# A graph layer on one core: whether nodes lie in a chunk's reach is told from each chunk's first and last edge, in the prologue, and no longer from all edges in the first passes

## The chip, the core and the metric

The program runs on one core of one Trainium2 chip. TensorE (PE; its weight loads are shown apart as PEld), VectorE (DVE), ScalarE (ACT) and GpSimd (POOL) compute; SyncE (SP) issues most of the plain DMAs, and POOL issues the indirect ones, which gather rows by an index in SBUF. The metric is the time of one execution on the device in microseconds, and of several executions the median. The profile is of one execution of its own.

## What is computed

One layer of a graph network on 12500 nodes of 128 features, with 200000 edges sorted by their target node `dst`. For each edge a score is taken between the target's query and the source's key and damped by `exp(-edge_weight)`; each node keeps its 16 best edges, makes a softmax of them, and adds up the messages of their sources.

```python
h = jnp.maximum(_layernorm(x, axis=-1), 0.0)
Qv = h @ W_Q.T
Ku = h @ W_K.T
score = jnp.einsum('md,md->m', Qv[dst], Ku[src]) * (1.0 / np.sqrt(d))
score = score * jnp.exp(-DECAY_LAMBDA * edge_dt)
order = jnp.lexsort((-score, dst))
...
keep = rank < TOPK
...
alpha = w / jnp.where(denom[dst_s] > 0, denom[dst_s], 1.0)
msgs = h[src_s] @ W_msg.T
agg = jax.ops.segment_sum(alpha[:, None] * msgs, dst_s, num_segments=n, indices_are_sorted=True)
return x + jax.nn.relu(h @ W_self.T + agg)
```

## The kernel before

**Groups and chunks.** The 200000 edges are cut into 1563 chunks of 128 edges, and 14 chunks (`GC`) are a group; there are 112 groups (`G`). A group answers for the nodes whose last edge lies in its 14 chunks, at most 128 nodes that follow one another. As the edges of its last node may run on, it also looks at the first chunk of the next group, so that it works on 15 chunks (`NJ`). A group's edges lie 128 to a chunk, one edge on each partition.

**The reach of a chunk.** Within its group, chunk j is taken to hold edges of the 40 nodes (`WN`) from place 8 j - 16 on, and no others. This is true of ordinary inputs but not of all, and so it is tested: places are told in `rel`, a tile with one group on each partition and, for each of its edges, the place of the edge's node among the group's nodes (112 x 1920, bf16). `w0` holds 8 j - 16 for each chunk. `dlw` is a view of `pd`, which has the same turned, with an edge on each partition: the place less the chunk's start, for 112 groups x 15 chunks, which makes 1680 elements on each of 128 partitions.

**What the tests lead to.** Tests write counts into the columns of `bad` (prologue) and of its copy `badc`: a node with 40 edges or more (column 0), `dst` not sorted (1), a node out of its chunk's reach (2), a group with too many nodes (3). `all_checked` adds them over the partitions with a small product on PE and writes `any_i`. At the end of the program (L904) all engines read `any_i`: if it is not 0, a general and much slower loop does the whole layer again.

**Prologue.** It loads the edges and `x`, writes `h` row by row into `h_tab` in DRAM, turns the indices of the sources into `idx_all`, builds `rel`, `pd` and the counts (L390 to L450). Tiles that only the prologue needs are in the pool `ep`, which ends with it; the pool `win` of the passes then lies in its place, so the first instruction that writes there waits for the last one that used `ep` (on ACT this is L539). POOL starts to gather rows here: for the first four groups (`RAW`) from `x`, to be normalised later, and for the others from `h_tab`.

**Gathers.** `let_go(g, k)` releases the gathers of two chunks: DVE copies two columns of indices into a small tile `ix` (L191), and POOL issues one indirect DMA for each chunk, 128 rows of 512 bytes into the tile `hs` of the group (L176). There are 8 buffers for `hs`, so a group's first gather also waits until PE has added up the group eight before it (L696), the last to read that buffer.

**Passes.** A loop over i from -3 to 110 does the work in an order written out by hand, and the engines run it as it stands, each its own instructions in that order. In pass i the stages of different groups stand side by side: nodes loaded for group i + 3, edges spread and places made for i + 1 (`far_of` L558, `away` L581, `places` L585), scores of i (L605) and their spread over slots (`scores_in_slots`, L613), slots of i - 1 gathered by node on PE (L621), best 16 of i - 2 (`best`, L635 on; `on_edges`, L670 to L677), weights and sums of i - 3 (L685, L686, L696), output of i - 5 (L716). `let_go` calls lie between them (`more`), mostly for groups i + 4 and i + 5. In passes 0 to 2 rows of groups 2 and 3 are normalised besides (L200, L221, L241).

**Work put off.** `later` is a list of small pieces of work. At the end of each pass with i > 0 one is taken from it:

```python
            if i > 0 and later:
                later.pop(0)()
```

Before the change there are nine, for passes 1 to 9. The first six tell whether nodes lie out of reach (L459, L471 to L475), all on DVE and all over the 1680 elements; the seventh and eighth are the count of edges per node (L477, L478), the ninth is `all_checked` (L463 to L467). The first six need two tiles of their own in `win`, `own_n` and `dl_n`.

Of the kernel before, what the change touches and what calls it, by code (L numbers as in the profile page):

```python
# [10 lines left out]
F32 = mybir.dt.float32  # L11
# [4 lines left out]
OP = mybir.AluOpType  # L16
# [4 lines left out]
P = 128  # L21
# [10 lines left out]
NJ = GC + 1  # L32
# [3 lines left out]
WN = 40  # L36
HALO = 64
# [23 lines left out]
def bc(ap, n):  # L61

    return ap.unsqueeze(2).to_broadcast([ap.shape[0], ap.shape[1], n])
# [7 lines left out]
def bm(ap, n):  # L71

    return ap.unsqueeze(1).to_broadcast([ap.shape[0], n, ap.shape[1]])
# [3 lines left out]
def gnn_layer(  # L77
# [27 lines left out]
    nc = tc.nc  # L105
    N, D = x.shape
# [5 lines left out]
    G = -(-CH // GC)  # L112
    assert G > TAIL + 2
    EG = GC * P
# [3 lines left out]
    RR = -(-CH // CPR)  # L118
# [28 lines left out]
    rel = const.tile([RR, RW + P], BF16, name="rel")  # L147
# [8 lines left out]
    dlw = pd[:, 16:16 + NJ, :].rearrange("e j g -> e g j")  # L156
# [88 lines left out]
    w0 = rows_pool.tile([P, NJ], F32, name="w0")  # L245
# [16 lines left out]
    with tc.tile_pool(name="edges", bufs=1) as ep, ExitStack() as stage:  # L262
# [8 lines left out]
        bad = ep.tile([P, 4], F32, name="bad")  # L271
# [29 lines left out]
        xs, t = [], 0  # L301
# [21 lines left out]
        k = RF if REM else RF - 1  # L323
# [21 lines left out]
        for w in range(2):  # L345
# [4 lines left out]
                                           op0=OP.mult, op1=OP.subtract)  # L350
# [27 lines left out]
        for g in range(2):  # L378
# [18 lines left out]
                                op0=OP.add, op1=OP.max)  # L397
# [7 lines left out]
        dst_f = dst_r.bitcast(F32)  # L405
# [11 lines left out]
        bb = rows_pool.tile([P, 2, G], F32, name="bb")  # L417
        nc.vector.tensor_copy(bb, pb[:, 0:2 * G].rearrange("p (a g) -> p a g", a=2))

        for j0 in range(0, NJ, 4):  # L420
            j1 = min(j0 + 4, NJ)
            pt = bank("q", 3)
            for j in range(j0, j1):
# [10 lines left out]
                                       op0=OP.add, op1=OP.is_gt, accum_out=bad[0:RR, 1:2])  # L434
# [4 lines left out]
        nc.vector.tensor_scalar(flags[:, 1:2], row[:, 0, G - TAIL:G - TAIL + 1], float(N - XT), None, op0=OP.is_lt)  # L439
        nc.vector.tensor_scalar(flags[:, 2:3], row[:, 0, G - TAIL - 1:G - TAIL], float(N - P), None, op0=OP.is_gt)  # L440
        nc.vector.tensor_reduce(bad[0:1, 3:4], flags[:, 0:3], axis=AX.X, op=OP.add)
        badc = rows_pool.tile([P, 4], F32, name="badc")
        nc.vector.tensor_copy(badc, bad)
        let_go(RAW, 6)
# [5 lines left out]
        nc.vector.tensor_copy(idxo, t1)  # L450


    mid = (WN - 1) / 2
    own_n, dl = [], []

    def far_from_start():
        for t in (own_n, dl):
            t.append(win.tile([P, G, NJ], F32, bufs=1, name="own_n" if t is own_n else "dl_n"))
        nc.vector.tensor_tensor(dl[0], dlw, bm(w0, G), op=OP.add)  # L459

    def all_checked():
        pb = bank("x", 1)
        nc.tensor.matmul(pb[0:1, 0:4], lhsT=ones, rhs=badc, start=True, stop=True)  # L463
        total = rows_pool.tile([1, 1], F32, name="total")
        nc.vector.tensor_reduce(total, pb[0:1, 0:4], axis=AX.X, op=OP.add)
        nc.vector.tensor_scalar(any_i, total, 1.0, None, op0=OP.min)
        nc.vector.tensor_scalar(uns, pb[0:1, 1:2], 1.0, None, op0=OP.min)  # L467

    later += [
        far_from_start,  # L470
        lambda: nc.vector.tensor_tensor(own_n[0], dl[0], bc(bb[:, 1, :], NJ), op=OP.is_lt),  # L471
        lambda: nc.vector.scalar_tensor_tensor(own_n[0], dl[0], 0.0, own_n[0], op0=OP.is_ge, op1=OP.mult),
        lambda: nc.vector.tensor_scalar(dl[0], dlw, -mid, None, op0=OP.add),
        lambda: nc.vector.tensor_tensor(dl[0], dl[0], dl[0], op=OP.mult),
        lambda: nc.vector.scalar_tensor_tensor(own_n[0], dl[0], (mid + 0.25) ** 2, own_n[0], op0=OP.is_gt,  # L475
                                               op1=OP.mult, accum_out=badc[:, 2:3]),
        lambda: nc.vector.tensor_reduce(badc[:, 0:1], pd[:, 0:NJ, :], axis=AX.XY, op=OP.max),  # L477
        lambda: nc.vector.tensor_scalar(badc[:, 0:1], badc[:, 0:1], float(KM), None, op0=OP.is_ge),  # L478
        all_checked,
# [424 lines left out]
    with tc.tile_pool(name="gen", bufs=1) as gen, tc.If(nc.values_load(  # L904
# [46 lines left out]
        lo, hi, clo, chi = row[:, 0, 0:NT], row[:, 0, 1:NB], row[:, 1, 0:NT], row[:, 2, 0:NT]  # L951
# [125 lines left out]
```

## Time and profile before

| | |
|---|---|
| median of 3 runs | 2030.86 us (2030.07 to 2034.2) |
| profiled execution | 2036.32 us, its span 2034.5 us |
| granted TensorE clock, mean | 0.915 |
| DVE busy | 1284.9 us, 63% |
| ACT busy | 1021.7 us, 50% |
| gathers (L176) from `h_tab` | 1507, first at 94.0 us, last at 1991.1 us |
| L459, one operation at 138.2 us | 3.23 us |
| L471, L472, L474, L475, one each from 156.2 to 212.4 us | 1.90 us each |
| L473, at 182.6 us | 1.71 us |
| L477, at 227.3 us | 1.90 us |

Times are microseconds from the span's start. In a list of groups, a line tells the program's line, the engine, the operation, the tile written and the tiles read, the shape, the count, then the busy time and the mean of one in ns, and the idle time of the engine just before these instructions with what ended most of it. "issue" as the cause means that the engine waited for nothing that the profile shows. In a timeline, a line has the start, the duration, engine, line, operation and tiles, and in brackets the idle time before it and what ended that.

### The profile page before, as it was taken

What the parts mean: (1) busy time and instruction counts of PE and PEld (TensorE: products, weight loads), DVE (VectorE), ACT (ScalarE), POOL (GpSimd) and SP (SyncE); (2) the same over time, 40 slices, a digit from 0 to 9 for tenths busy, and PEclk for the clock granted to TensorE, in tenths of its full rate; (3) what the DMA queues carried; (4) which work ended last, traced back from release to release, by engine and by line L of the source; (5) the groups of instructions that cost most, each with busy time, mean ns of one, the idle gap of its engine ahead of it and who ended that gap; (6) DMA issues with size and microseconds to landing.
All of it is one profiled execution on the core that took longest, in us unless ns stands there. A gap on an engine that the chain in (4) does not pass through costs nothing. (4 is left out here: it accounts for less than half of the span.)

```text
span 2034.5 us, 42215 instructions
## 1 busy us (share of the span) xinstructions
PE 1580.1 (78%) x13800; PEld 1303.9 (64%) x13801; DVE 1284.9 (63%) x7017; ACT 1021.7 (50%) x2190; POOL 1505.6 (74%) x1580
## 2 busy tenths in 40 slices
PE   0268899977878787888878787778878787878785
PEld 0147777766666666666666666666666666666664
DVE  7568877756656666666666566666666665666653
ACT  5765566544444454454444445444544444545440
POOL 6777777777777777777777777777777777777772
PEclk9979999998889899998888899898988888989987
DMA  9522222222222222222222222222222222222220
GB/s 220 179 59 56 76 69 69 66 64 66 65 65 66 65 64 63 66 65 65 66 65 66 66 65 64 64 64 65 66 66 65 65 66 66 66 64 64 64 58 19
DMA packets 101472, 143.46 MB, mean 71 GB/s; under 512 B 31063, under 2 KB 74327, under 8 KB 100480
## 3 DMA queue, kind: packets, MB, share of 16 engines
q0 software_dynamic: 50144, 102.74, 19.9%
q1 hardware_dynamic: 51102, 37.99, 6.8%
q8 instruction: 108, 1.77, 0.4%
q14 instruction: 118, 0.97, 0.2%
HBM read 126.79 MB, written 14.40 MB: 69 GB/s over the span
## 5 line engine op out<-in xcount | busy, mean ns | idle before, releaser
L176 POOL DMA_INDIRECT hs<-h_tab,ix x1507 | 1436.4, 953 | 461.9 <-issue 304.6
L605 DVE SCALAR_TENSOR_TENSOR prod<-hs,dec_all,q 128x128 f32<-128x128 f32 x1674 | 507.6, 344 | 296.2 <-DMA hs<-h_tab,ix 256.8
L558 ACT ACTIVATE far<-a,minus 128x512 bf16<-128x512 f32 (+1 forms) x447 | 294.3, 658 | 530.8 <-PE a L556 523.7
L596 PE MATMUL q<-q,to_e 128*128 128x128 f32 x3348 | 512.4, 301 | 0.0
L596 PEld LDWEIGHTS q<-q,to_e 128*128 128x128 f32 x3348 | 482.6, 213 | 33.5 <-DVE prod L605 13.7
L696 PE MATMUL e<-hs,alz 128*128 128x128 f32 x3240 | 419.1, 282 | 0.0
L696 PEld LDWEIGHTS e<-hs,alz 128*128 128x128 f32 x3240 | 377.9, 192 | 26.9 <-issue 19.2
L581 ACT ACTIVATE aw<-a 128x400 bf16<-128x400 f32 x336 | 169.1, 503 | 314.3 <-PE a L579 314.3
L635 DVE TENSOR_SCALAR ell<-slots,e 128x40 f32<-128x40 f32 x112 | 28.1, 251 | 357.1 <-PE e L621 304.6
L704 PE MATMUL s<-ident,agn 128*128 128x128 f32 x112 | 38.3, 342 | 262.8 <-DVE kept L685 260.8
L563 ACT ACTIVATE to_e<-far 128x1920 f32<-128x1920 bf16 x112 | 201.4, 1798 | 3.5
L556 PE MATMUL a<-rel,ident 112*128 112x512 bf16 (+1 forms) x447 | 195.0, 436 | 8.2 <-ACT far L558 8.1
L704 PEld LDWEIGHTS s<-ident,agn 128*128 128x128 f32 x112 | 17.0, 152 | 279.0 <-issue 274.7
L621 PE MATMUL e<-opo,sl 128*41 128x40 f32 x3348 | 194.0, 233 | 0.0
L621 PEld LDWEIGHTS e<-opo,sl 128*41 128x41 f32 x3348 | 180.1, 147 | 12.3
L605 DVE DVE_READ_ACCUMULATOR prod<-hs,dec_all,q 128x1 f32 x1674 | 138.4, 83 | 0.0
L585 ACT ACTIVATE opo<-aw 128x1200 f32<-128x1200 bf16 x112 | 134.2, 1198 | 0.1
L191 DVE COPY ix<-idx_all 128x2 int32<-128x2 int32 x754 | 133.2, 192 | 0.0
L579 PE MATMUL a<-minus_at,pdT 32*128 32x400 bf16 x336 | 115.4, 343 | 19.3 <-ACT pdT L572 9.6
L664 PE MATMUL x<-km,to_e 128*128 128x43 bf16 x1674 | 61.1, 183 | 66.7 <-DVE km L647 66.0
L664 PEld LDWEIGHTS <-to_e 128*128 128x128 bf16 x1674 | 49.7, 97 | 98.3 <-DVE km L647 96.7
L613 DVE TENSOR_TENSOR sl<-opo,s 128x600 f32<-128x600 f32 x112 | 87.6, 782 | 4.0
(179 smaller groups left out, 1678.0 us busy)
## 6 DMA issues: line engine op xcount, KB each, us to landing
hs<-h_tab,ix POOLq DMA_INDIRECT x1507
h_r<-h_tab SPq DMA_DIRECT2D x112, 64.0 KB
x_t<-in_x_dram SPq DMA_DIRECT2D x108, 64.0 KB
out_dram<-o SPq DMA_DIRECT2D x108, 64.0 KB
xg<-in_x_dram SPq DMA_DIRECT2D x2, 1400.0 KB
h_tab<-xg SPq DMA_DIRECT2D x2, 1400.0 KB
xg<-in_x_dram SPq DMA_DIRECT2D x1, 1120.0 KB
h_tab<-xg SPq DMA_DIRECT2D x1, 1120.0 KB
```

The lines of the kernel that those rows point to most:

```text
L176: nc.gpsimd.indirect_dma_start(out=T[g]["hs"][:, j, :], out_offset=None, in_=table[0:N, :], in_offset=bass.IndirectOffsetOnAxis(ap=index(j ...
L191: nc.vector.tensor_copy(ix[:, j0:j1], idx_all[:, GC * g + j0:GC * g + j1])
L556: nc.tensor.matmul(pr[:, 0:n1 - n0], lhsT=upper(ident[0:RR, g:g + 1]).to_broadcast([RR, P]), rhs=rel[:, n0:n1], start=True, stop=True)
L558: nc.scalar.activation(T[g]["far"][:, n0:n1], pr[:, 0:n1 - n0], AF.Square, bias=minus)
L563: nc.scalar.activation(T[g]["to_e"][:, 0:n], T[g]["far"][:, 0:n], AF.Relu, bias=1.0, scale=-1.0)
L579: nc.tensor.matmul(pr[:, 0:400], lhsT=T[g]["pdT"], rhs=minus_at.rearrange("k w j s -> k (w j s)")[:, n0:n1], start=True, stop=True)
L581: nc.scalar.activation(T[g]["aw"][:, n0:n1], pr[:, 0:400], AF.Square)
L585: nc.scalar.activation(T[g]["opo"].rearrange("e w j s -> e (w j s)"), T[g]["aw"], AF.Relu, bias=1.0, scale=-1.0)
L596: nc.tensor.matmul(pq[:, (j - j0) * P:(j - j0 + 1) * P], lhsT=T[g]["to_e"][:, j * P:(j + 1) * P], rhs=T[g]["q"], start=True, stop=True)
L605: nc.vector.scalar_tensor_tensor(prod, rows_of(g, j), dec_all[:, c:c + 1], T[g]["pq", b][:, (j % 4) * P:(j % 4 + 1) * P], op0=OP.mult, op1 ...
L621: nc.tensor.matmul(et[0:KM + 1, STEP * j:STEP * j + WN], lhsT=sl1[g % 2][:, j, :], rhs=T[g]["ow"][:, j, :], start=False, stop=(j == n - 1))
L696: nc.tensor.matmul(T[g]["pa"], lhsT=alz[g % 2][:, WW * j + PRE:WW * j + PRE + P], rhs=rows_of(g, j), start=(j == 0), stop=(j == n - 1))
```

## The change

The six operations on all edges go, and with them the tiles `own_n` and `dl_n`. In their place eleven small DVE operations stand in the prologue, between the other counts and the copy of `bad` to `badc`. As the edges are sorted, the places within a chunk never fall, so that the first and last edge of each chunk bound them. For each group (a partition) and chunk (15 elements) the new code takes the places of these two edges from `rel`, cuts them to the group's own nodes and the nodes that there are (`at_most`), and compares them with the chunk's start `w0` and with the start plus 40. Chunks that begin past the group's last node don't count. The number of chunks out of reach goes into column 2 of `bad`. The list `later` keeps three pieces, which are now due in passes 1, 2 and 3 and no longer in passes 7, 8 and 9.

```diff
         nc.vector.tensor_reduce(bad[0:1, 3:4], flags[:, 0:3], axis=AX.X, op=OP.add)
+        ends = rel.rearrange("g (j p) -> g j p", p=P)
+        lo, hi = ends[:, :, 0], ends[:, :, P - 1]
+        at_most = ep.tile([RR, 2], F32, name="at_most")
+        below, out_of = (ep.tile([RR, NJ], F32, name=f"out_of{k}") for k in range(2))
+        nc.vector.tensor_scalar(at_most[:, 0:1], dst_f[:, HALO - 1:HALO], -1.0, float(N - 2), op0=OP.mult, op1=OP.add)
+        nc.vector.tensor_copy(at_most[:, 1:2], rel[:, EG - 1:EG])
+        nc.vector.tensor_tensor(at_most[:, 0:1], at_most[:, 0:1], at_most[:, 1:2], op=OP.min)
+        nc.vector.tensor_scalar(out_of, hi, at_most[:, 0:1], None, op0=OP.min)
+        nc.vector.tensor_tensor(out_of, out_of, w0[0:RR, :], op=OP.subtract)
+        nc.vector.tensor_scalar(out_of, out_of, WN - 0.5, None, op0=OP.is_gt)
+        nc.vector.tensor_scalar(below, lo, 0.0, None, op0=OP.max)
+        nc.vector.tensor_tensor(below, below, w0[0:RR, :], op=OP.subtract)
+        nc.vector.scalar_tensor_tensor(out_of, below, 0.0, out_of, op0=OP.is_lt, op1=OP.max)
+        nc.vector.tensor_scalar(below, lo, at_most[:, 0:1], None, op0=OP.is_le)
+        nc.vector.scalar_tensor_tensor(out_of, out_of, 1.0, below, op0=OP.mult, op1=OP.mult,
+                                       accum_out=bad[0:RR, 2:3])
         badc = rows_pool.tile([P, 4], F32, name="badc")
         nc.vector.tensor_copy(badc, bad)
         let_go(RAW, 6)
...
-    mid = (WN - 1) / 2
-    own_n, dl = [], []
-
-    def far_from_start():
-        for t in (own_n, dl):
-            t.append(win.tile([P, G, NJ], F32, bufs=1, name="own_n" if t is own_n else "dl_n"))
-        nc.vector.tensor_tensor(dl[0], dlw, bm(w0, G), op=OP.add)
...
     later += [
-        far_from_start,
-        lambda: nc.vector.tensor_tensor(own_n[0], dl[0], bc(bb[:, 1, :], NJ), op=OP.is_lt),
-        lambda: nc.vector.scalar_tensor_tensor(own_n[0], dl[0], 0.0, own_n[0], op0=OP.is_ge, op1=OP.mult),
-        lambda: nc.vector.tensor_scalar(dl[0], dlw, -mid, None, op0=OP.add),
-        lambda: nc.vector.tensor_tensor(dl[0], dl[0], dl[0], op=OP.mult),
-        lambda: nc.vector.scalar_tensor_tensor(own_n[0], dl[0], (mid + 0.25) ** 2, own_n[0], op0=OP.is_gt,
-                                               op1=OP.mult, accum_out=badc[:, 2:3]),
         lambda: nc.vector.tensor_reduce(badc[:, 0:1], pd[:, 0:NJ, :], axis=AX.XY, op=OP.max),
         lambda: nc.vector.tensor_scalar(badc[:, 0:1], badc[:, 0:1], float(KM), None, op0=OP.is_ge),
         all_checked,
```

## The prediction

> **What bounds the kernel now.** I read the page's groups first, then the timeline of POOL, and only then the engines that feed it.
>
> ```profile
> PE 1580.1 (78%) x13800; PEld 1303.9 (64%) x13801; DVE 1284.9 (63%) x7017; ACT 1021.7 (50%) x2190; POOL 1505.6 (74%) x1580
> ...
> L176 POOL DMA_INDIRECT hs<-h_tab,ix x1507 | 1436.4, 953 | 461.9 <-issue 304.6
> ```
>
> PE is busier than POOL, but the busy share misleads. A gather (L176) takes 953 ns with 461.9 / 1507 = 0.31 us of idle before it that is put down to "issue", that is, to nothing but POOL itself. Together 1.25 us each. 1507 of them are 1898 us (1436.4 + 461.9), 93% of the span. The POOL timeline shows where this stream is not at that beat; the columns are start, duration, engine, line, operation, tiles and the idle time before it:
>
> ```profile
> 139.48 2.74 POOL L176 DMA_INDIRECT hs<-h_tab,ix  x1 [0.30 <-issue]
> ...
> 156.25 2.64 POOL L176 DMA_INDIRECT hs<-h_tab,ix  x1 [0.30 <-DVE hs L241]
> ...
> 166.71 0.94 POOL L176 DMA_INDIRECT hs<-h_tab,ix  x1 [0.30 <-issue]
> 168.91 1.19 POOL L176 DMA_INDIRECT hs<-h_tab,ix  x1 [1.25 <-PE a L579]
> 171.97 1.00 POOL L176 DMA_INDIRECT hs<-h_tab,ix  x1 [1.87 <-issue]
> ...
> 182.01 2.41 POOL L176 DMA_INDIRECT hs<-h_tab,ix  x1 [0.30 <-DVE prod L605]
> ...
> 197.75 2.42 POOL L176 DMA_INDIRECT hs<-h_tab,ix  x1 [0.30 <-DMA hs<-h_tab,ix]
> ...
> 213.51 1.58 POOL L176 DMA_INDIRECT hs<-h_tab,ix  x1 [0.30 <-issue]
> ```
>
> Two things are to be seen. Some gathers take 2.4 to 2.7 us and not 0.94. And after 171.97 no gather has more than 0.31 us of idle before it up to the last, at 1991.09: from there **POOL alone sets the time**. The stores at the end wait for DVE's work on the last gathered rows, a tail of 2034.5 - 1992.0 = 42.5 us that the change does not touch. So a microsecond taken from a gather after 169 us ends the program a microsecond earlier; one taken before 169 has to pass the wait of 1.25 us at 168.91. What stood beside the long gathers is in the timeline of DVE:
>
> ```profile
> 103.33 0.35 DVE L605 SCALAR_TENSOR_TENSOR prod<-hs,dec_all,q 128x128 f32<-128x128 f32 x1 [18.15 <-ACT opo L585]
> ...
> 138.22 3.23 DVE L459 TENSOR_TENSOR dl_n<-pd,w 128x1680 f32<-128x1680 bf16 x1
> ...
> 169.27 1.90 DVE L472 SCALAR_TENSOR_TENSOR own_n<-dl_n,own_n 128x1680 f32<-128x1680 f32 x1
> ```
>
> **What is removed.** Six operations on 1680 elements, one at the end of each of passes 1 to 6. Each with the gather beside it (start and duration from the two timelines), and what that gather lost against 0.94:
>
> - L459, 138.22, 3.23 us: gather 139.48 took 2.74, loss 1.80
> - L471, 156.18, 1.90: gather 156.25 took 2.64, loss 1.70
> - L472, 169.27, 1.90: the gather of 168.91 took 1.19 and the next began at 171.97; 171.97 - 168.91 - 1.25 = 1.81
> - L473, 182.59, 1.71: gather 182.01 took 2.41, loss 1.47
> - L474, 197.45, 1.90: gather 197.75 took 2.42, loss 1.48
> - L475, 212.38, 1.90: gather 213.51 took 1.58, loss 0.64
>
> The gathers end 0.8 us behind the end of the DVE operation (156.18 + 1.90 = 158.08 against 158.89; 199.35 against 200.17): they are held, not slowed. I take that as a shared path to SBUF.
>
> **The rule that speaks against it.** The Trainium skill, "SBUF — State Buffer", section "Who interferes with whom", says that a VectorE operation with two SBUF inputs contends with GpSimd's reads, but infers that it leaves descriptor generation alone, which needs the write side; its probe saw tensor_tensor stall no DMA. By that, five of the six (all with two inputs) cost POOL nothing, only L473 is left, and the sum is 1.47: 2029.4, no change. The rows say 2.64 and 2.42 beside just such operations, and 0.94 a few gathers on. I go by the rows. The same section says that a reduce never contends; I use that for L477 below, where the row is ambiguous.
>
> **What of it counts.** The first two losses, 3.50 us, lie before 168.91. That gather is the first of group 8 and takes group 0's buffer, so it must wait until PE has summed group 0:
>
> ```profile
> 166.31 2.05 PE L696 MATMUL e<-hs,alz 128*128 128x128 f32 x16
> 168.30 0.34 PE L579 MATMUL a<-minus_at,pdT 32*128 32x400 bf16 x1
> ```
>
> The sums end at 168.36 and the gather starts 0.55 later; POOL had been ready at 167.65 + 0.30 = 167.95. Are the sums earlier without L459 and L471? DVE was idle 0.94 us before 142.39 and 1.07 us before 160.05, waiting for PE (L621), just after these two operations; and the weights that the sums read were done at 158.98, 4.0 us before PE took them at 163.01. The chain runs through PE and ACT (ACT has one gap of 0.28 us from 141.11 to 149.97). So I count **nothing for L459 and L471**: the wait grows from 1.25 to 1.25 + 3.50 = about 4.8 us. The other four sum to 1.81 + 1.47 + 1.48 + 0.64 = **5.4 us**, all after the wait.
>
> Does POOL then run into the next wait? Group 9's first gather would come 14 x 1.25 = 17.5 after 168.91, at 186.4. Its index copy was done at 180.99, and PE's sums of group 1 before 181.76, when ACT had the product behind them: about 5 us of margin. The index copies of group 8's second and third pair were done at 169.36 and 172.29, and would be needed at 171.4 and 173.9. Passes 4 to 7 last 14.9 us with these operations and 13.3 without (start to start of L613), against 17.5 for POOL's 14 gathers, so the margin grows.
>
> Six shorter losses remain in the same stretch: 0.55, 0.57, 0.58, 0.48, 0.30 and 0.35 at 184.72, 211.70, 226.63, 229.71, 255.15 and 256.70, sum 2.83. The first four start within 0.2 us behind L613 or L686 (0.78 us, two inputs each), which stay, but at another time. In the ten passes from 257 to 390, at 13.3 us each, such losses sum to 0.36 + 0.18 + 0.45 + 0.44 = 1.43, or 0.14 a pass; six passes at that rate are 0.86 and the gain 2.0. At worst they fall as before, gain 0. I take the middle, 1.0.
>
> **What is added.** Eleven DVE operations on 1 or 15 elements a partition, before the copy to badc at 83.57. Rows near it: 0.17 for 14 elements (L219), 0.22 (L447), with 0.03 to 0.2 between dependent ones; so 0.14 to 0.24 each, about 2.2 us together (1.5 to 2.6). DVE then is idle for 18.15 us, so the cost is **zero**. Queued behind them: the index copy at 83.65, whose gather starts at 108.97; the other copies from 84.39, later still; and ACT's L539 at 89.75, the first to write where these tiles lay, which would have to wait for about 86.7. Without that idle time it would be 2.2 us. No DMA is added, and neither SP nor POOL is passed.
>
> **What is moved.** L477 (reduce, 1.90) goes from pass 7 to pass 1, in L459's place; there a loss of up to 1.8 on POOL would vanish in the wait. In pass 7 it stood beside a gather that lost 0.58, but L613 began 0.08 before that gather, as it did at 211.70 where L475 had not begun, so I have counted it with the short ones. L478 (0.15) goes to pass 2. The final sum, a small PE product and three DVE operations of 0.14 to 0.15, goes from pass 9 to pass 3: PE gets there at about 169.1, its bank having been read by 166.8, DVE is free at 169.3, so it waits for perhaps 0.1 and is done near 169.9, where L472 ended at 171.17. Zero.
>
> **Sum.** 5.4 + 1.0 = 6.4 us. The profiled execution took 2036.3 (span 2034.5), 5.5 above the median 2030.86; the terms are absolute and I take them off the median: **2024.5 us**. A difference of 0.2% (4.1 us) is about the least that can be told from none.
>
> **Rivals.**
>
> - *The early losses count too, 0.20.* If the sums of group 0 come earlier after all, up to 3.5 more, and with the short losses gone 5.4 + 2.8 + 3.5 = 11.7: 2019.2; its middle 2021.5. For it: the wait was only 0.96 too long. Against: DVE idles on PE just behind both operations.
> - *The loss comes back, 0.21.* The gathers lose their time in smaller pieces to L613, L675 and L686, which a compute loop of 13.3 us brings by more often, or the rule above holds: 0 to 4 gained, 2028.5. For it: short operations took 2.8 us in six passes. Against: only 1.4 in the next ten.
> - *A worse lock, 0.09, the slower side.* In the steady state a pass lasts as long as 14 gathers, 17.5 us, so L613 or L686 meets POOL at the same phase each time. Were that phase a bad one, each pass would lose 0.55. It eats the gain from 6.4 / 0.55 = 12 passes on, and is slower by 0.2% from 19; at 30 it is 2030.9 - 6.4 + 16.5 = 2041. Against: DVE's phase follows from the rows' landing, as before, where 1300 us cost POOL only 1.2.
> - *The new test flags the input* and the general path runs: below 0.01. For these inputs the farthest node lies 32 places past its chunk's start (limit 39) and the nearest 9 (limit 0), worked out from the reference's data.
>
> **Chances.** The forecast has 0.50, and of it 0.43 lie beyond 4.1 us. Faster: 0.43 + 0.20 = 0.63; same: 0.07 + 0.20 + 0.01 = 0.28; slower: 0.08 of the lock and 0.01 of the second rival, 0.09. The range from 2019.5 (nearly everything counts) to 2031 (nothing, with the spread of the shown runs, 2030.07 to 2034.2, in part) leaves out the lock and the last of the first rival.
>
> **What would show it.** Right: no gather over 1.6 us from 100 to 260 us; some 4.8 us of idle before the gather near 168.9, which starts where it did; the last gather at about 1991.1 - 6.4 = 1984.7, and an unchanged tail. Wrong: that gather starting well before 168; gathers of over 2 us beside other operations; many of 1.5 us after 400 us; a tail that is longer; ACT's L539 after 90 us.

## The result, and the profile after

| | before | after |
|---|---|---|
| median of 12 runs | 2031.65 us (2028.43 to 2035.7) | 2025.11 us (2021.62 to 2028.43) |
| ratio after / before, 95% interval | | 0.9964 (0.9956 to 0.9972) |
| profiled execution, its span | 2036.32, 2034.5 us | 2026.79, 2025.0 us |
| gathers, mean | 953 ns | 949 ns |

The change made the kernel 6.5 us faster by the medians; 2024.5 us had been forecast. The ratio is estimated from all executions and is not the quotient of the two medians: it makes 7.3 us, and its interval 5.7 to 8.9. Line numbers are now higher, by 18 behind the prologue's tests and by 3 from L482 on (L605 became L608, L613 L616, L686 L689, L696 L699).

The group of the gathers on the page:

```profile
L176 POOL DMA_INDIRECT hs<-h_tab,ix x1507 | 1430.8, 949 | 464.0 <-issue 291.9
```

The gathers' busy time fell by 5.6 us, the idle time before them rose by 2.1: the kernel is still a stream of gathers. POOL's timeline, at the wait and at the two latest gathers behind it within 60 us:

```profile
160.74 0.94 POOL L176 DMA_INDIRECT hs<-h_tab,ix  x1 [0.31 <-issue]
164.80 1.20 POOL L176 DMA_INDIRECT hs<-h_tab,ix  x1 [3.11 <-PE a L582]
167.86 0.95 POOL L176 DMA_INDIRECT hs<-h_tab,ix  x1 [1.87 <-issue]
...
191.64 1.12 POOL L176 DMA_INDIRECT hs<-h_tab,ix  x1 [0.30 <-issue]
...
218.13 1.47 POOL L176 DMA_INDIRECT hs<-h_tab,ix  x1 [0.30 <-issue]
```

The gathers of 2.4 to 2.7 us are gone, and the idle time before group 8's first gather has grown from 1.25 to 3.11 us. But the 1.87 us before its second gather, which the prediction gave to L472, stand there unchanged, without L472. DVE's timeline has the new operations (their first and last, and the next score):

```profile
80.00 0.13 DVE L448 TENSOR_SCALAR at_most<-dst_r 112x1 f32<-112x1 f32 x1
...
81.87 0.17 DVE L458 SCALAR_TENSOR_TENSOR out_of<-out_of,out_of 112x15 f32<-112x15 f32 x1
...
99.86 0.35 DVE L608 SCALAR_TENSOR_TENSOR prod<-hs,dec_all,q 128x128 f32<-128x128 f32 x1 [15.86 <-ACT opo L588]
```

They take 2.1 us, and DVE's idle time behind them went from 18.15 to 15.86.

**How two executions are compared.** The two spans differ by 9.5 us, more than the medians. I cut each POOL timeline at group 8's first gather. The beat is what the starts of neighbouring gathers are usually apart. "Late" is what they are apart beyond the beat, summed over those that are over 0.06 us late.

| us | before | after | difference |
|---|---|---|---|
| start of the prologue's row counts (L391), before anything changed | 67.77 | 64.18 | -3.6 |
| from there to group 8's first gather | 101.14 | 100.62 | -0.5 |
| late, from group 8's third gather on | 9.86 | 4.61 | -5.2 |
| beat of 1449 gathers (1248.5 and 1251.0 ns) | | | +3.6 |
| last gather's start to the end | 43.44 | 39.69 | -3.8 |

The first row lies ahead of everything that changed. The beat differs as much between the changed kernel's two profiles (1251.0 and 1248.4 ns). The last row goes with the granted TensorE clock. PE adds up a group of the last passes so, before and after:

```profile
1998.30 5.14 PE L696 MATMUL a<-hs,alz 128*128 128x128 f32 x30 [0.20 <-DVE alz L686]
...
1991.43 3.62 PE L699 MATMUL a<-hs,alz 128*128 128x128 f32 x30 [0.20 <-DVE alz L689]
```

In the 22 us from the last gather's start the mean granted clock was 0.92 before and 1.00 after. Of the twelve profiles of this study with a clock of 0.89 to 0.92 over the whole program, five have 1.00 there and a tail of 39.4 to 40.2 us, seven have 0.90 to 0.92 and a tail of 42.3 to 43.6 us. One of the five is the kernel before with three of the six operations, one of the seven the changed kernel without its prologue operations, so the tail does not go with the change. What the change can have done is in the second and third row.

### The profile page after: what moved, and what is told of

Read it like the earlier page. It is cut to its first block, busy times and chain, and to the rows that moved or that the text cites. A ratio compares the mean times of both kernels' runs of the same rounds, so it can differ in the third digit from the quotient of the medians.

```text
span 2025.0 us, 42221 instructions
## 1 busy us (share of the span) xinstructions
PE 1571.0 (78%) x13800; PEld 1297.0 (64%) x13801; DVE 1274.4 (63%) x7022; ACT 1023.3 (51%) x2190; POOL 1500.8 (74%) x1580
## 5 line engine op out<-in xcount | busy, mean ns | idle before, releaser
L608 DVE SCALAR_TENSOR_TENSOR prod<-hs,dec_all,q 128x128 f32<-128x128 f32 x1674 | 507.9, 344 | 300.0 <-DMA hs<-h_tab,ix 259.0
L699 PE MATMUL e<-hs,alz 128*128 128x128 f32 x3240 | 419.0, 282 | 0.0
L699 PEld LDWEIGHTS e<-hs,alz 128*128 128x128 f32 x3240 | 377.9, 191 | 26.9 <-issue 19.2
L624 PE MATMUL e<-opo,sl 128*41 128x40 f32 x3348 | 189.0, 230 | 0.0
L624 PEld LDWEIGHTS e<-opo,sl 128*41 128x41 f32 x3348 | 175.3, 144 | 12.1
L608 DVE DVE_READ_ACCUMULATOR prod<-hs,dec_all,q 128x1 f32 x1674 | 138.1, 82 | 0.1
L616 DVE TENSOR_TENSOR sl<-opo,s 128x600 f32<-128x600 f32 x112 | 87.6, 782 | 4.0
```

The source lines that it names most:

```text
L608: nc.vector.scalar_tensor_tensor(prod, rows_of(g, j), dec_all[:, c:c + 1], T[g]["pq", b][:, (j % 4) * P:(j % 4 + 1) * P], op0=OP.mult, op1 ...
L624: nc.tensor.matmul(et[0:KM + 1, STEP * j:STEP * j + WN], lhsT=sl1[g % 2][:, j, :], rhs=T[g]["ow"][:, j, :], start=False, stop=(j == n - 1))
L699: nc.tensor.matmul(T[g]["pa"], lhsT=alz[g % 2][:, WW * j + PRE:WW * j + PRE + P], rhs=rows_of(g, j), start=(j == 0), stop=(j == n - 1))
```

## The experiments

### Which of the six operations cost time

**All six taken out** of the kernel before, and nothing put in their place:

```diff
     later += [
-        far_from_start,
-        lambda: nc.vector.tensor_tensor(own_n[0], ...
...
+        lambda: None,
...
```

> The kernel before with the six operations of passes 1 to 6 replaced by nothing, the rest of the put-off work in its old passes 7 to 9, and no prologue operations: the test of the reach is left out. Theory (gathers held by these operations, after POOL's wait at the first gather of group 8): the whole gain of the change is here, 5 to 7.5 us below the kernel before, no gather over 1.6 us between 170 and 260 us. Rival (the gain comes from the pieces that move from passes 7 to 9 to passes 1 to 3, or from the placing of tiles): under 2 us.

**The first two kept**, the other four `lambda: None`:

> The same, but L459 and L471 stay in passes 1 and 2; their result is not used, and the test of the reach is left out. Theory: their two gathers take 2.6 to 2.8 us, but the wait at group 8's first gather takes it in (idle before it about 1.3 and not about 4 us), so the time is that without them, 5 to 7.5 us below the kernel before. Rival (early losses count): 3.5 us slower than without them, 2 to 4 us below the kernel before.

**L473 to L475 kept**, the first three `lambda: None` (L475 reads `dl_n` twice, as `own_n` has no value then, and its sum is left out):

> The same, but of the six only L473, L474 and L475 stay, in passes 4 to 6; their result is not used, and the test of the reach is left out. Theory as the two traces now have it (L472 costs nothing, since the 1.87 us of idle before group 8's second gather is there without it too): 3.6 us of held gathers and up to 2 us of short ones remain, so 0 to 2.5 us below the kernel before. The prediction as it was written (L472 costs 1.8): 1.8 us or more below it. Rival (the late ones cost nothing at the end, it is the early ones): 5 us or more below it.

**The changed kernel without its eleven operations:**

```diff
-        ends = rel.rearrange("g (j p) -> g j p", p=P)
...
-                                       accum_out=bad[0:RR, 2:3])
```

> The changed kernel without its eleven operations in the prologue: the test of the reach is left out. Theory (DVE is idle behind them): the time of the changed kernel, 5.5 to 7.5 us below the kernel before. Rival (they delay the first passes): 2 us better still, 8 us or more below it.

**The changed kernel once more:**

> The changed kernel once more, to see what differs between executions of one kernel. Theory: after the wait at group 8's first gather the same gathers are late at the same distance from it up to 500 us; the prologue and the tail differ by up to 4 us. Time 5.5 to 7.5 us below the kernel before. Rival (the late gathers fall anew each time): other places and sums.

Medians against the kernel before on the same chip, and the parts of each kernel's one profiled execution, worked out from POOL's timeline as above (gather 420 of those from `h_tab` starts at about 630 us):

| kernel | median, us | ratio (95%) | L391 | L391 to group 8 | idle before group 8 | late before it | late behind it, to gather 420 | late, the rest | last gather to end |
|---|---|---|---|---|---|---|---|---|---|
| before | | | 67.77 | 101.14 | 1.25 | 4.05 | 8.67 | 1.19 | 43.44 |
| none of the six | -2.2 | 0.9982 (0.9973 to 0.9991) | 66.29 | 100.50 | 4.57 | 0.15 | 3.99 | 2.58 | 43.10 |
| first two only | -6.1 | 0.9964 (0.9951 to 0.9977) | 65.65 | 100.48 | 1.19 | 3.54 | 3.51 | 0.00 | 42.28 |
| L473 to L475 only | -2.3 | 0.9988 (0.9980 to 0.9997) | 66.38 | 99.95 | 3.63 | 0.56 | 8.37 | 0.06 | 39.42 |
| changed, no prologue operations | -4.5 | 0.9970 (0.9961 to 0.9980) | 67.42 | 99.67 | 3.62 | 0.22 | 3.49 | 1.68 | 42.73 |
| changed | -6.5 | 0.9964 (0.9956 to 0.9972) | 64.18 | 100.62 | 3.11 | 0.10 | 3.45 | 1.16 | 39.69 |
| changed, again | -5.8 | 0.9971 (0.9960 to 0.9983) | 65.48 | 100.72 | 5.79 | 0.24 | 3.44 | 2.00 | 39.58 |

In us, the ratios make 3.7, 7.3, 2.4, 6.1, 7.3 and 5.9 below the kernel before, in the order of the table. What the late gathers behind the wait are fewer than before (9.86) makes 3.3, 6.3, 1.4, 4.7, 5.2 and 4.4. So each kernel gains what the late gathers of its one profile say, and 0.4 to 2.1 us more, which I can't place.

With the first two alone the whole gain is there, although nothing is added in the prologue and the last three pieces stay in passes 7 to 9.

The early two cost nothing. Their gathers are late (136.68 takes 3.39 us), and the wait takes it in; the kernel with the first two only:

```profile
136.68 3.39 POOL L176 DMA_INDIRECT hs<-h_tab,ix  x1 [0.30 <-DVE ix L191]
...
166.13 1.19 POOL L176 DMA_INDIRECT hs<-h_tab,ix  x1 [1.19 <-PE a L578]
169.20 0.95 POOL L176 DMA_INDIRECT hs<-h_tab,ix  x1 [1.87 <-issue]
```

and that with none of the six:

```profile
166.79 1.19 POOL L176 DMA_INDIRECT hs<-h_tab,ix  x1 [4.57 <-PE a L578]
169.85 0.95 POOL L176 DMA_INDIRECT hs<-h_tab,ix  x1 [1.88 <-issue]
```

From L391, group 8's first gather starts after 100.48 and 100.50 us: 3.4 us of held gathers move nothing but the idle time, 1.19 against 4.57.

L473 to L475 bring the late gathers back, 8.37 against 3.99 us up to gather 420. The kernel with these three:

```profile
179.38 2.52 POOL L176 DMA_INDIRECT hs<-h_tab,ix  x1 [0.30 <-DVE prod L607]
...
195.25 2.42 POOL L176 DMA_INDIRECT hs<-h_tab,ix  x1 [0.31 <-DVE ix L191]
...
211.01 1.58 POOL L176 DMA_INDIRECT hs<-h_tab,ix  x1 [0.30 <-issue]
```

Its gain, 0.6 to 4.1 us by the interval, lies clear of the 4.7 to 10.0 of the kernel with the first two. From that with none of the six (1.8 to 5.5) the times alone do not tell it. L472 is not in it, and 8.37 of the 8.67 us remain, so L472 holds 0.3 us of them at most. The eleven operations cost nothing that shows in the time: without them the gain is 4.5 us, with them 5.8 and 6.5. Group 8's first gather comes 1 us sooner without them, but kernels that have them differ by more (99.39 us from L391 in that with a reduce, below).

In the changed kernel's two profiles the late gathers are the same ones as long as they come soon after the wait. The second one:

```profile
166.20 1.20 POOL L176 DMA_INDIRECT hs<-h_tab,ix  x1 [5.79 <-PE a L582]
169.27 0.95 POOL L176 DMA_INDIRECT hs<-h_tab,ix  x1 [1.87 <-issue]
...
192.99 1.24 POOL L176 DMA_INDIRECT hs<-h_tab,ix  x1 [0.30 <-issue]
...
219.48 1.51 POOL L176 DMA_INDIRECT hs<-h_tab,ix  x1 [0.30 <-issue]
```

192.99 - 166.20 = 26.8 and 219.48 - 166.20 = 53.3 us, as 26.8 and 53.3 in its first profile. I take it that the wait sets POOL and the passes to the same phase each time. The likeness ends 187 us behind the wait, where 500 us had been expected; behind gather 420 the sums are 1.16 and 2.00.

One thing did not come as expected: with none of the six the median is only 2.2 us below the kernel before, and not 5 to 7.5. The changed kernel, whose late gathers up to gather 420 come to within 0.5 us of its, gains 5.8 to 6.5. The kernel with none of the six ran once more, and the kernel before with it (the 4.7 us in the text are those up to gather 420):

> The kernel before without the six operations once more (the test of the reach is left out), since its first median lay only 2.2 us below the kernel before, where the sum of its late gathers says 4.7. Theory (the sum is right, the first median was drawn high): 3.5 to 6 us below the kernel before. Rival (its placing of the work costs 2 to 3 us somewhere else): 1 to 3 us below it again.

> The kernel before once more, for what differs between executions: within 1.5 us of its own median. Theory: after group 8's first gather the same gathers are late as in its first profile, at the same distance (13.1, 15.8, 28.8, 42.8, 44.6 us and so on), 8.6 us together up to gather 420; the prologue and the tail differ. Rival: other places, and a sum that differs by over 1 us.

These two ran where TensorE had a granted clock of 0.75 (0.89 to 0.92 in all other profiles), and all took 3100 us: 3096.88 against 3099.75 before, ratio 0.9990 (0.9978 to 1.0001), and 3100.57 for the kernel before, 1.0007 (0.9998 to 1.0015). So they answer neither question, but another one. The kernel before, there:

```profile
L176 POOL DMA_INDIRECT hs<-h_tab,ix x1507 | 1450.5, 962 | 1467.6 <-PE e L696 580.6
```

and one of its waits, with the gather behind it on time:

```profile
802.50 0.95 POOL L176 DMA_INDIRECT hs<-h_tab,ix  x1 [4.18 <-DVE prod L605]
803.76 0.94 POOL L176 DMA_INDIRECT hs<-h_tab,ix  x1 [0.30 <-issue]
```

POOL is idle for 1467.6 us before the gathers: 580.6 are put down to PE, which has to free buffers, and 407.5 to DVE's L605. So POOL alone no longer sets the time, and what is taken from a gather can be lost at the next such wait, as it was before group 8. That the operations are gone gives nothing there that can be told from zero. What made these executions slow is open. It was not the clock alone: the prologue's row counts (L391) start at 97.15 us and not at 67.77, though the granted clock was 1.00 up to there.

For the first run of the kernel with none of the six the table has most of the answer. Behind the wait it has 6.57 us of late gathers in all, against 4.61 and 5.44 in the changed kernel and 3.51 in that with the first two, and 2.58 of them come after gather 420. By these it should gain 3.3 us; the median says 2.2 and the ratio 3.7. Why more gathers are late in it than in the others stays open.

### What holds a gather

One DVE operation more at the end of each of 80 passes of the changed kernel, in four forms; the tiles take the room of `own_n` and `dl_n`, and nothing reads the results:

```diff
                 later.pop(0)()
+            if i == 24:
...
+                nc.vector.memset(probe_a, 0.0)
+            if 25 <= i < 105:
+                nc.vector.tensor_tensor(probe_b, probe_a, probe_a, op=OP.mult)
```

> The changed kernel with one more DVE operation at the end of each of the passes 25 to 104, of L474's form: 1680 elements, f32, both inputs in SBUF; its result is not used. Theory (a gather waits until such an operation ends): 0.64 to 1.8 us a pass as the rows of the kernel before, so 50 to 145 us more than the changed kernel, and some 80 gathers of over 1.5 us. Rival (the Trainium skill's inference that such an operation leaves descriptor generation alone): 0 to 10 us more, as DVE has room for 1.9 us in a pass.

The other three have, in place of the last line, a `tensor_reduce` of `pd` as in L477, a `tensor_scalar` of `dlw` as in L473, and a `tensor_copy` of `probe_a`.

> The same with a reduce of L477's form (1680 bf16 elements, one input, 1.90 us). Theory (the loss beside L477 came from L613 and L686): 0 to 8 us more than the changed kernel. Rival (any long DVE operation holds a gather): 50 us more or above.

> The same with a tensor_scalar of L473's form (1680 elements, one bf16 input with a stride, f32 out, 1.71 us). Theory (L473 held its gather by 1.47 us): 50 to 120 us more than the changed kernel. Rival (one input and no faster mode do not hold; L473's gather was held by L686 or L613 beside it): 0 to 10 us more.

> The same with a copy of 1680 f32 elements from SBUF to SBUF. Theory (it runs in a two-port mode in about 1.1 us and holds a gather for that time, less what the gather's own gap covers): 0.3 to 1 us a pass, 25 to 80 us more than the changed kernel. Rival (it is too short to hold a gather): 0 to 10 us more.

| form, 1680 elements | one takes, us | median against the kernel before (95% of the ratio) | gathers that end 0.8 us behind it | that end 0.1 us behind it |
|---|---|---|---|---|
| two f32 inputs | 1.91 | +100.1 (1.0457 to 1.0522) | 80 of 80 | 0 |
| reduce of bf16 | 1.90 | +25.4 (1.0092 to 1.0152) | 0 | 0 |
| one bf16 input, stride | 1.68 | +113.9 (1.0526 to 1.0589) | 47 | 33 |
| copy f32 | 1.04 | +64.5 (1.0281 to 1.0348) | 49 | 31 |

Against the changed kernel each is some 6.5 us more, if it gains on this chip what it gained above (it was not run here): 107, 32, 120 and 71. The reduce meets neither of its forecasts. A pass with a two-input operation, in the timeline of all engines, POOL's and the added line alone:

```profile
696.40 1.90 DVE L824 TENSOR_TENSOR probe_b<-probe_a 128x1680 f32<-128x1680 f32 x1
696.48 2.64 POOL L176 DMA_INDIRECT hs<-h_tab,ix  x1 [0.30 <-issue]
```

The gather starts 0.08 us behind the operation and ends at 699.12, 0.82 us behind its end at 698.30; and so in all 80. A gather that is already running is not held by it: 22 were, and none of them ended later for it. The copy holds too:

```profile
712.48 1.03 DVE L824 COPY probe_b<-probe_a 128x1680 f32<-128x1680 f32 x1
712.58 1.75 POOL L176 DMA_INDIRECT hs<-h_tab,ix  x1 [0.30 <-issue]
```

But the copy and the strided one-input form also hold a gather that is already running, until 0.12 us behind their own end (31 and 33 of 80; a few of these began up to 0.03 us after the operation). So L473's form does the same as the copy, and the gather beside L473 in the kernel before was such a one:

```profile
182.59 1.71 DVE L473 TENSOR_SCALAR dl_n<-pd 128x1680 f32<-128x1680 bf16 x1
```

It began at 182.01, before L473, and ended 0.12 behind it, at 184.42.

The reduce holds none of its 80. And yet it cost 32 us. Its timeline, with L616, L689 and POOL:

```profile
755.39 0.79 DVE L616 TENSOR_TENSOR sl<-opo,s 128x600 f32<-128x600 f32 x1
756.16 1.90 DVE L824 TENSOR_REDUCE probe_b<-pd 128x1 f32<-128x1680 bf16 x1
756.16 0.94 POOL L176 DMA_INDIRECT hs<-h_tab,ix  x1 [0.30 <-issue]
757.41 0.94 POOL L176 DMA_INDIRECT hs<-h_tab,ix  x1 [0.30 <-DMA hs<-h_tab,ix]
758.37 0.78 DVE L689 TENSOR_TENSOR alz<-opo,kept 128x600 f32<-128x600 f32 x1
758.66 1.31 POOL L176 DMA_INDIRECT hs<-h_tab,ix  x1 [0.30 <-issue]
```

Two gathers pass beside the reduce in 0.94 us each. But it has pushed L689, 0.78 us with two inputs, to where a gather starts 0.29 us behind it, and that one is late. Of the 112 operations of L689 it happens to 81 here, 27.8 us together; without the reduce (the changed kernel) to 3, 1.3 us, since gathers start 0.6 us or more behind L689, when it is nearly done. In the changed kernel's two profiles, too, the late gathers start 0.05 to 0.55 us behind the start of L616 or L689, and end 0.82 us behind its end.

### The wait at group 8

> The changed kernel with a ninth buffer for gathered rows, in the room that own_n and dl_n left (used by group 8 alone), and with group 8's and all later index copies released one pass earlier. Theory (POOL's wait for the sums of group 0, and the 1.81 us that the gather behind it loses in every trace so far, are time of the whole program): no idle over 0.4 us between 100 and 260 us, and 2.8 + 1.8 = 4.6 us less than the changed kernel, 9.5 to 12 us below the kernel before. Rival 1 (the 1.81 us belong to the first use of a buffer again and not to the wait): 2.8 us less. Rival 2 (short operations of DVE then meet POOL at a worse phase): no gain or a loss.

```diff
         if j0 == 0:
-            T[g]["hs"] = rows_pool.tile([P, GC, D], F32, name="hs", bufs=8)
+            if g == 8:
+                T[g]["hs"] = win.tile([P, GC, D], F32, bufs=1, name="hs_ninth")
+            else:
+                T[g]["hs"] = rows_pool.tile([P, GC, D], F32, name="hs", bufs=8)
...
-                if i in (-1, 0, 1):
+                if i in (-1, 0, 1, 2):
                     g = i + 6
                 else:
-                    g, k = (i + 4, k + 2) if k < 5 else (i + 5, k - 5)
-                    if g < 8:
+                    g, k = (i + 5, k + 2) if k < 5 else (i + 6, k - 5)
+                    if g < 9:
                         return
```

Its median is 2021.92 us, 11.0 below the kernel before (ratio 0.9946, 0.9933 to 0.9960), and 5.1 below the changed kernel on the same chip (2027.03). POOL at group 8:

```profile
163.40 0.95 POOL L179 DMA_INDIRECT hs<-h_tab,ix  x1 [0.30 <-issue]
164.65 0.94 POOL L179 DMA_INDIRECT hs_ninth<-h_tab,ix  x1 [0.30 <-DMA hs<-h_tab,ix]
165.90 0.95 POOL L179 DMA_INDIRECT hs_ninth<-h_tab,ix  x1 [0.30 <-issue]
167.16 1.40 POOL L179 DMA_INDIRECT hs_ninth<-h_tab,ix  x1 [0.30 <-DVE prod L611]
```

Neither the wait nor the 1.87 us behind it are there. From L391 it is 97.67 us to group 8's first gather, 3.0 less than in the changed kernel, and the second gather follows 1.81 us sooner: 4.8, as expected (4.6) and near the 5.1 measured. The 1.81 us come and go with the wait at group 8: in all thirteen other profiles of this study the gather behind it is 1.81 or 1.82 late, whatever DVE does beside it. They belong neither to a buffer that is used again (here group 9 is the first to do so, and its second gather is on time) nor to every wait: where the clock was 0.75, POOL waited over 2 us some 200 times in each profile, and the gather behind was late by 1.8 at group 8 and on time at nearly all the others, as at 803.76 above. What makes them is open. This is the fastest version here; its two parts were not tried apart.

## Why the prediction was right, step by step

- **POOL alone sets the time behind 169 us: right.** With the two-input operation in 80 passes, the late gathers of these passes sum to 106.6 us, and the time rose by 100.1 + 6.5. Where TensorE's clock was 0.75 it does not hold: POOL waits there over 2 us some 200 times, and taking out the six operations gains nothing that can be told from zero.
- **L459 and L471 count nothing: right**, as the kernel that keeps them shows. The wait grew to 3.1 in one profile and 5.8 in another (4.8 forecast), by when the prologue let POOL start. One sign of being wrong that the prediction names seems to have come, as group 8's first gather starts at 164.80 and so well before 168; but the prologue itself ran 3.6 us earlier, and from L391 the gather comes 0.5 us sooner.
- **L472 costs 1.81: wrong.** This term of the sum was mis-sized: without L472 the 1.81 us were there unchanged, and what it held of the other late gathers is 0.3 at most. I saw L472 in the time between two gathers and took it for the cause. The 1.81 us come with the wait, and the wait stayed. The kernel after shows it without an experiment.
- **L473 to L475 cost 1.47 + 1.48 + 0.64: right.** Alone they bring back gathers that are 1.57, 1.47 and 0.63 late, at 13.1, 28.9 and 44.7 us behind group 8's first. The prediction's reading that the gathers end 0.8 us behind the operation does not hold for L473, where it is 0.12. And part of that gather's lateness has another cause: with none of the six it is still 0.56 late, beside L613 (L612 there).
- **The short losses give 1.0: low.** Up to gather 420 the kernel before has 8.67 us of late gathers, of which 8.67 - 3.57 = 5.10 are not beside the three operations; the changed one has 3.45 and 3.44. That is 1.65. Part of it is the moved work: wherever `all_checked` stands in pass 9, two gathers 81 to 88 us behind group 8's first are late by 0.3 and 0.35; in the changed kernel's first profile one is there, 0.28 late at 80.1 us.
- **The sum.** 5.4 + 1.0 became 3.6 + 1.65 = 5.2: one term was 1.81 too high, the other 0.65 too low. The medians say 6.5 and 5.8. The intervals are 5.7 to 8.9 and 3.5 to 8.1, so 5.2 lies just below the first and inside the second; the remaining 0.6 to 1.3 us I can't place. That the median came within 0.7 us of the forecast is so in part luck: the late gathers show less gain than was summed, and the rest that fills it up was not foreseen. (Two middles that the rivals name are 0.4 us off: 2021.5 should be 2021.9, and 0 to 4 us gained has its middle at 2028.9.)
- **The tail is unchanged: not as profiled**, 39.69 us against 43.44; but the difference goes with the granted clock and not with the change.
- **The prologue's operations are hidden: right**, 2.1 us for the 2.2 forecast; ACT's L539, now L542, came at 86.30 with no wait for them.
- **The rule against the change.** The Trainium skill, "SBUF — State Buffer", section "Who interferes with whom", infers that a two-input operation leaves the making of descriptors alone. If that is to mean that such an operation costs these gathers nothing, it fails: 80 of 80 were held. The section also says that a two-input operation contends with a GpSimd instruction that reads SBUF. That agrees with a gather that is held at its start only, if it reads its indices there, which no run here shows. Of a reduce it says that on this chip it never contends, and 0 of 80 were held. Of an operation in a mode that takes both ports it says that it blocks the other engine fully, and that a copy can enter such a mode: the copy also holds a running gather (31 of 80), and its 1.04 us against the reduce's 1.90 for as many elements speak for such a mode. The strided one-input form holds just so, but takes 1.68 us; whether it takes both ports is not shown.
- **The rival with a worse phase was not this change's case, but it is real**: of the 32 us that the reduce cost, which itself holds nothing, 27.8 came through it, 0.34 us in each of 81 passes.

## What to carry to other kernels

Where GpSimd's gathers set the time, as here, ask of a VectorE operation not only how long it is but whether a gather starts or runs beside it. In these runs a two-input operation held a gather that started beside it until it ended, a copy and a one-input operation with a stride also held one that was running, and a reduce held none but pushed the next two-input operation onto a gather. Before a held gather is counted as time, look for the next wait of the gather stream: what is lost ahead of it came free here. And an operation that stands in a gap is not its cause until the gap is seen to go with it: here gap and wait went together, with one more buffer.

## What the runs showed that I had not expected

- Group 8's second gather comes 1.81 to 1.82 us late in thirteen profiles, 0.00 in the one without the wait in front of it, and nearly all other waits do not have it.
- In the changed kernel's two profiles the late gathers repeat for 187 us behind the wait, within 0.1 us in place and 0.12 us in size, so that collisions that look like chance are a property of the kernel there.
- The same program can take 3100 us and not 2031. The granted TensorE clock is then 0.75 and PE's L696 takes 416 ns and not 282, but the prologue is 29 us later too, before the clock falls. POOL no longer sets the time alone, and what does is open.
